# Early transposes of h0: a four-layer graph network on one Trainium2 core, with 64 small transposes moved to its start

## The chip, the cores and the metric

The kernel runs on 1 core of one Trainium2 chip. The metric is the device time of one execution in microseconds (us), and the kernel before takes 1860.86 us, the median of 3 runs (1860.08 to 1861.27). Its engines are named as the profile names them: PE does matmuls (PEld loads their weights), DVE is VectorE, ACT is ScalarE, POOL is GpSimd, and SP issues most transfers (its rows are named SPq). Each works through its own instructions in order.

## The reference

6,250 nodes with 128 features, 206,250 edges sorted by their target (every node has a loop), and four graph layers in a row, each added to x. What matters here is the first:

```python
h = jnp.maximum(_layernorm(x, axis=-1), 0.0)
msg = edge_weight[:, None] * h[src]
neighbor = segment_sum(msg, dst, num_segments=6250)
interaction = h * neighbor
out = neighbor @ W1.T + b1 + interaction @ W2.T + b2
x = x + leaky_relu(out, 0.2)
```

The second layer takes the mean of the neighbours' normed rows, the third a mean over another table's rows by the same edges, the fourth a gated recurrent cell on the neighbours' sum. All use the same edges, so one dense matrix of edge counts serves them.

## The kernel before, in words

The nodes are padded to NB = 49 blocks of 128. The edges are turned into dense matrices, and every sum over neighbours is then a matmul. The kernel has four parts.

**The head.** x is loaded in groups of GB = 4 blocks, normed in place into the tile h0 (128 rows x 49 blocks x 128 features, kept on the chip), and the edges of the first strip are fetched. `normed(n)` (L894) does n groups' norms.

**The strips.** 25 strips of SB = 2 blocks of target nodes (`strip`, L938; the last has one block). A strip has 32 *counts* (`count`, L766). A count is 24 bf16 matmuls (L781) of one-hot columns (`one_hots`, L747, DVE) into a PSUM tile pK, and two ACT copies out of it: L790 writes the edge counts as bytes to `cnt`, L788 the summed edge weights to `edge_w`. Finished counts are stored to DRAM (`cnt_d`, L969) for the later layers. `edge_w` is 49 x 256 f32 a partition. Strips take it in turn from two pools of one buffer each, edge0 for even strips and edge1 for odd ones (L940).

Between the counts of strip k stands the work of earlier strips, as generators that the loop calls at fixed places (the tables END_AT, EDGES_AT, NORMS_AT in L932 to L936). The instructions run in exactly this order, because `manual_schedule` (L886) is on:
- `layer0(k-1)` (L810): the first layer's sum, h0 times `edge_w`, as f32 matmuls of half the rows each into the two PSUM tiles pB and pM (L818). It comes in 16 *turns*, one after every second count. Then ACT copies pB to `agg` (L826) and DVE adds pM (L827).
- `finish0(k-2)` (L842), a strip's *end*: `turned_rows` (L833) transposes h0's two blocks as four 64 x 64 pieces (L839) into a PSUM tile pt. DVE multiplies it by `agg` into `inter` (L848). Eight matmuls by W1 and W2 (L855, L856) follow, then bias, leaky relu, the next norm, four transposes of the new rows h1 by the same L839, and a matmul (L876). h1, the new x and that product go to DRAM (h_d, u_d, f_d).

The small tiles of the ends (agg, inter, xs0, full, h1, ht0, fs) come from the pool `work` (L614), which is opened ahead of edge0 and edge1 (L615), pay, hot, cnts, turned and once (L633, L634). So their size decides at which address the others begin. After the last strip the remaining turns of `layer0` run by themselves, with the last full strip's end spread between them (L1008 to L1012).

**The dense layers.** The strips' pools are closed with their `with` block. New pools take the same space from its start: late, work, late2, ring (3 buffers), wide (3), early, whole (4), in L1016 to L1022. Layer 2's `dense` (L1025) works in steps of five blocks of source nodes. In `bring` (L1031), SP loads byte counts into a `ring` tile (L1051, 640 KB for two steps), DVE (L1066) and ACT (L1064) widen them to `wide`, a row for each block, and PE multiplies each row by the block's `parts`, the high and low half of h1 (L1088, two matmuls a row). `parts` is filled by `h_up_to` (L1136): POOL loads a group of h1 from h_d into one of four `h` tiles of the pool whole (L1141), DVE casts it to the high half (L1151), and the low half is a subtraction on DVE or, from group 7 on, POOL (L1152).

The scheduler decides how these late instructions stand between those of the last strips. One that writes space of a closed pool waits for the last reader of what lay there.

Of the kernel before, what the change touches and what calls it, by code (L numbers as in the profile page):

```python
# [488 lines left out]
NPR = -(-NB // 2)  # L489
NBP = 2 * NPR  # L490
KP = 5
KQ = 5
NSMP = -(-E // P)
TOP = 1 << 13
# [5 lines left out]
def fast(ctx: ExitStack, tc: tile.TileContext, a: dict, out: bass.AP, flag: bass.AP):  # L500
# [33 lines left out]
    f_d = dram.tile([P, NB, D], F32, name="f_d")  # L534
    h_d = dram.tile([P, NB, D], F32, name="h_d")
    x_d = dram.tile([P, NB, D], F32, name="x_d")
    smp_d = dram.tile([NSMP, 1], I32, name="smp_d")

    def rows(table, g, nb):
# [57 lines left out]
    with ExitStack() as bx:  # L597
# [149 lines left out]
        def one_hots(by_edge, t0):  # L747

            of = slice(t0 // TI, t0 // TI + tq)
            keys, parts = (t[:, of, :, None, :] for t in by_edge)  # L750

            def at(i, n):
                return keys[:, :, i].to_broadcast([P, tq, n, TI])

            def count_up(n):
                return iota[:, None, :n, :].to_broadcast([P, tq, n, TI])

            s_hot = hot.tile([P, tq, P, TI], BF16, name="s_hot")
            nc.vector.tensor_tensor(s_hot, count_up(P), at(0, P), op=ALU.is_equal)  # L759
            k_hot = hot.tile([P, tq, 4, NBP, TI], BF16, name="k_hot")  # L760
            nc.vector.tensor_tensor(k_hot[:, :, 0], count_up(NBP), at(1, NBP), op=ALU.is_equal)  # L761
            nc.vector.tensor_tensor(k_hot[:, :, 1:, :NB], k_hot[:, :, :1, :NB].to_broadcast([P, tq, 3, NB, TI]),  # L762
                                    parts.to_broadcast([P, tq, 3, NB, TI]), op=ALU.mult)
            return s_hot, k_hot
# [45 lines left out]
        def layer0(k, nb, edge_w):  # L810

            g, w = k * SB, nb * P
            pl = [psum.tile([P, 512], F32, name=n) for n in ("pB", "pM")]
            for i in range(turns0):
                for s in range(i * NB // turns0, (i + 1) * NB // turns0):
                    for h in range(WN):
                        r = slice(h * H, (h + 1) * H)
                        nc.tensor.matmul(pl[h][:, :w], h0[r, s, :], edge_w[r, s, :w], start=s == 0,  # L818
                                         stop=s == NB - 1)
                if i + 1 < turns0:  # L820
                    yield
            if k == NS - 1:
                ends.append(pl)
                return
            agg = work.tile([P, SW], F32, name="agg")
            nc.scalar.copy(agg[:, :w], pl[0][:, :w])  # L826
            nc.vector.tensor_add(agg[:, :w], agg[:, :w], pl[1][:, :w])  # L827
            ends.append(finish0(g, nb, agg))

        def by_half(t, nb):  # L830
            return t[:, : nb * P].rearrange("p (b h c) -> p h b c", h=WN, c=H)

        def turned_rows(t, nb):  # L833

            pt = banks.tile([P, WN, 512], F32, name="pt", tag="pK")
            for j in range(nb):
                for h in range(WN):
                    r = slice(h * H, (h + 1) * H)
                    nc.tensor.transpose(pt[:, h, j * H : (j + 1) * H], t[r, j, :], ident[r, r])  # L839
            return pt[:, :, : nb * H].rearrange("p h (b c) -> p h b c", c=H)  # L840

        def finish0(g, nb, agg):  # L842

            w = nb * P
            queue = nc.sync if g < (NS - 3) * SB else nc.gpsimd
            pt = turned_rows(h0[:, g : g + nb, :], nb)
            inter = work.tile([P, SW], F32, name="inter")
            nc.vector.tensor_mul(by_half(inter, nb), by_half(agg, nb), pt)  # L848
            xs = work.tile([P, SB, D], F32, name="xs0", bufs=2)
            load_x(xs, g, nb)  # L850
            yield
            po = banks.tile([P, SW], F32, name="po", tag="pK")
            for j in range(nb):
                s = slice(j * P, (j + 1) * P)
                nc.tensor.matmul(po[:, s], agg[:, s], w1, start=True, stop=False)  # L855
                nc.tensor.matmul(po[:, s], inter[:, s], w2, start=False, stop=True)  # L856
            full = work.tile([P, SW], F32, name="full")
            nc.vector.tensor_add(full[:, :w].rearrange("p (b f) -> p b f", f=D),
                                 po[:, :w].rearrange("p (b f) -> p b f", f=D), bcast(b12, nb))
            nc.vector.scalar_tensor_tensor(full[:, :w], full[:, :w], 0.2, full[:, :w],  # L860
                                           op0=ALU.mult, op1=ALU.max)
            nc.vector.tensor_add(flat(xs[:, :nb, :]), flat(xs[:, :nb, :]), full[:, :w])
            h1 = work.tile([P, SB, D], F32, name="h1")
            yield from norm(xs, h1, nb)
            nc.gpsimd.tensor_tensor(xs[:, :nb, :], xs[:, :nb, :], h1[:, :nb, :], op=ALU.add)
            queue.dma_start(h_d[:, g : g + nb, :], h1[:, :nb, :])
            queue.dma_start(u_d[:, g : g + nb, :], xs[:, :nb, :])
            yield
            pt = turned_rows(h1, nb)
            ht = work.tile([P, SW], F32, name="ht0")  # L870
            nc.scalar.copy(by_half(ht, nb), pt)
            yield
            pf = banks.tile([P, SW], F32, name="pf", tag="pK")
            for j in range(nb):
                s = slice(j * P, (j + 1) * P)
                nc.tensor.matmul(pf[:, s], ht[:, s], wr, start=True, stop=True)  # L876
            fs = work.tile([P, SB, D], F32, name="fs")
            nc.vector.tensor_add(fs[:, :nb, :], pf[:, :w].rearrange("p (b f) -> p b f", f=D),
                                 bcast(bl, nb))
            queue.dma_start(f_d[:, g : g + nb, :], fs[:, :nb, :])  # L880
# [13 lines left out]
        def normed(n):  # L894
            for _ in range(2 * n):
                next(norming)

        first = prepare(0)
        next(first)
        normed(4)  # L900
        next(first)
        normed(1)
        next(first)
# [22 lines left out]
        by_edge = next(first)  # L926
        next(norming)
        hots = one_hots(by_edge, 0)
        before, ends, turns, edges = iter(()), [], turn(), prepare(1)


# [6 lines left out]
        def strip(k, nb):  # L938
            nonlocal before, edges, by_edge, hots
            edge_w = edge[k % 2].tile([P, NB, SW], F32, name="edge_w")  # L940
            end = ends.pop() if ends else iter(())
            last, piece, following = nb * P // WN, 0, None
            for w0 in range(0, last, PW):
                if w0 % TW == 0:
                    if k < 2 and piece in NORMS_AT[k]:
                        next(norming, None)
                    if not k and piece in FIRST_AT:
                        following = next(edges, None)
                    now, t1 = hots, w0 + TW
                    if t1 < last:  # L950
                        hots = one_hots(by_edge, t1)
                    elif following:
                        hots = one_hots(following, 0)
                if w0 // PW % PT == PT // 2:
                    if piece in END_AT:
                        next(end, None)
                    if k < 2 and piece in NORMS_AT[k]:
                        next(norming, None)
                    if k and piece in EDGES_AT:
                        following = next(edges, None)  # L960
                if w0 * WN % P == 0:
                    cnt = cnts.tile([P, NPR, P], U16, name="cnt")
                count(w0, now, cnt, edge_w)
                if k and w0 // PW % 2:
                    next(before, None)
                g, w1 = k * SB + w0 * WN // P, w0 + PW
                if w1 * WN % P == 0:
                    c, i = CHUNK_OF[g]
                    nc.sync.dma_start(cnt_d[c, :, i, :], flat(cnt))  # L969
                if w1 % (PW * PT) and w1 < last:  # L970
                    continue
                if piece == (NEXT_AT if k else FIRST_AT[-1]) and k + 2 < NS:
                    edges = prepare(k + 2)
                    next(edges)
                for _ in range(TURN_AT.count(piece) if k else 0):
                    next(turns, None)
                piece += 1
            by_edge = following
            for _ in before:
                next(end, None)  # L980
            for _ in end:
                pass
            before = layer0(k, nb, edge_w)
# [601 lines left out]
```

## Time and profile before

| what | value |
|---|---|
| runs, median of 3 | 1860.86 us |
| the profiled execution, its own time | 1859.0 us |
| its span (first to last instruction) | 1857.2 us |
| granted PE clock | 0.994 |
| PE busy | 1791.2 us (96%) |
| DVE, ACT, POOL busy | 1381.6, 1208.7, 471.6 us |
| L818, the first layer's sums | 4900 matmuls, 1237.0 us on two row halves that run side by side |
| L781, the counts | 18816 matmuls, 404.5 us |
| L1088, the dense layers | 2548 matmuls, 574.3 us |
| L839, the transposes in the ends | 192, median 219 ns |

The time is 1.8 us above the span of the same execution. Busy time of one engine can overlap that of another. Two row halves of PE also overlap, so PE's busy time is not the sum of its rows. A profile row reads: line, engine, operation, the tile written, an arrow, the tiles read, the count, then the shape.

### The profile page before, as it was taken

The numbers are of one execution on the slowest core, as the hardware profiler recorded it, in microseconds if no ns is written. First come the engines' busy times: TensorE is split into PE (matmuls) and PEld (weight loads), VectorE is DVE, ScalarE is ACT, GpSimd is POOL, SyncE is SP. The second block draws the span as 40 slices with busy tenths as digits, with TensorE's granted clock in tenths as the row PEclk, the third lists the DMA queues.
The fourth block names the chain that finished last, engine by engine and source line by source line (L and its number), as shares of the span: only waits on it lengthen the run. The fifth ranks groups of instructions, "written<-read, shape, count | busy, mean of one in ns | idle before, by whom it ended". The sixth has DMA issues, their size and how long they took to land. (4 is left out here: it accounts for less than half of the span.)

```text
span 1857.2 us, 65339 instructions
## 1 busy us (share of the span) xinstructions
PE 1791.2 (96%) x28191; PEld 1521.2 (82%) x28191; DVE 1381.6 (74%) x2946; ACT 1208.7 (65%) x2835; POOL 471.6 (25%) x431
## 2 busy tenths in 40 slices
PE   2799999999999999999999999999999999999997
PEld 2688888888888888888888888888888877787776
DVE  7878888888888888888886777777787755454444
ACT  6777777777777777777774677777565654443443
POOL 2333333433334333334332111111122210000000
PEclk9899999999999999999999999999999999999999
DMA  4245454644644544545223555554555444344342
GB/s 106 58 123 115 101 139 106 129 126 100 136 106 118 122 103 126 117 99 132 72 79 117 179 173 162 167 154 124 143 155 147 139 148 142 121 136 148 121 140 60
DMA packets 262513, 231.72 MB, mean 125 GB/s; under 512 B 101518, under 2 KB 246424, under 8 KB 262215
## 3 DMA queue, kind: packets, MB, share of 16 engines
q1 hardware_dynamic: 253415, 210.67, 42.4%
q0 software_dynamic: 8800, 16.78, 3.2%
q8 instruction: 223, 3.65, 0.8%
q14 instruction: 75, 0.61, 0.1%
HBM read 130.37 MB, written 76.54 MB: 111 GB/s over the span
## 5 line engine op out<-in xcount | busy, mean ns | idle before, releaser
L818 PE MATMUL pM<-edge_w,h 64*128 64x256 f32 (+1 forms) x2450 | 619.2, 387 | 0.2
L818 PE MATMUL pB<-edge_w,h 64*128 64x256 f32 (+1 forms) x2450 | 617.8, 387 | 0.7 <-ACT agg L826 0.3
L1088 PE MATMUL acc<-wide,parts 128*128 128x512 f32 (+2 forms) x2548 | 574.3, 383 | 2.7 <-DVE wide L1066 1.3
L1088 PEld LDWEIGHTS acc<-wide,parts 128*128 128x128 f32 x2548 | 460.0, 188 | 101.2 <-issue 10.5
L790 ACT CAST cnt<-pK 128x400 uint8<-128x400 f32 x784 | 394.9, 504 | 222.5 <-PE pK L781 187.4
L781 PEld LDWEIGHTS <-s_hot 64*128 64x128 bf16 x18816 | 382.9, 95 | 80.5 <-issue 21.5
L818 PEld LDWEIGHTS pB<-edge_w,h 64*128 64x128 f32 x2450 | 421.6, 187 | 31.5 <-issue 3.3
L781 PE MATMUL pK<-k_hot,s_hot 64*128 64x49 bf16 (+1 forms) x18816 | 404.5, 192 | 32.2 <-DVE k_hot L762 19.2
L818 PEld LDWEIGHTS pM<-edge_w,h 64*128 64x128 f32 x2450 | 421.6, 187 | 5.4 <-issue 2.9
L788 ACT COPY edge_w<-pK 128x392 f32<-128x392 f32 x784 | 397.0, 506 | 0.0
L759 DVE TENSOR_TENSOR s_hot<-iota,keys 128x2048 bf16<-128x2048 bf16 x196 | 240.7, 1228 | 85.5 <-remote 52.5
L762 DVE TENSOR_TENSOR k_hot<-k_hot,by_edge 128x2352 bf16<-128x2352 bf16 x196 | 271.6, 1386 | 8.4
L1066 DVE TENSOR_SCALAR_CACHE_REDUCE wide<-ring 128x512 fp32r<-128x512 uint8 (+2 forms) x325 | 193.4, 651 | 25.3 <-issue 15.6
L1064 ACT ACTIVATE wide<-ring 128x512 fp32r<-128x512 uint8 (+2 forms) x312 | 184.7, 595 | 24.3 <-ACT wide L1064 19.6
L639 POOL DMA_INDIRECT dst<-in_dst,off_i x50 | 84.1, 1682 | 360.7 <-DVE node L702 341.6
L1058 ACT CAST wide<-ring 128x1024 fp32r<-128x1024 uint8 (+3 forms) x130 | 120.7, 957 | 70.6 <-PE acc L1088 65.7
L1057 DVE CAST wide<-ring 128x1536 fp32r<-128x1536 uint8 (+2 forms) x130 | 119.6, 945 | 53.4 <-PE acc L1088 41.5
L1088 PE MATMUL acc<-wide,q_parts 128*128 128x512 f32 (+2 forms) x650 | 157.3, 392 | 1.2 <-DVE wide L1043 0.9
L1088 PEld LDWEIGHTS acc<-wide,q_parts 128*128 128x128 f32 x650 | 115.6, 188 | 28.5 <-DVE wide L1043 3.1
L761 DVE TENSOR_TENSOR k_hot<-iota,keys 128x800 bf16<-128x800 bf16 x196 | 112.4, 573 | 0.0
L1429 POOL DMA_DIRECT2D out<-x x12 | 10.2, 853 | 322.9 <-DVE x L1426 293.1
L639 POOL DMA_INDIRECT line<-in_dst,at_i x24 | 40.9, 1703 | 163.2 <-DVE at_i L675 155.3
(246 smaller groups left out, 1650.3 us busy)
## 6 DMA issues: line engine op xcount, KB each, us to landing
ring<-cnt_d SPq DMA_DIRECT2D x110, 640.0 KB
cnt_d<-cnt SPq DMA_DIRECT2D x49, 800.0 KB
cntT_d<-tt SPq DMA_DIRECT2D x125, 160.0 KB
ring<-cntT_d SPq DMA_DIRECT2D x60, 320.0 KB
ring<-cnt_d SPq DMA_DIRECT2D x10, 480.0 KB
ring<-cnt_d SPq DMA_DIRECT2D x10, 320.0 KB
h<-in_x SPq DMA_DIRECT2D x12, 256.0 KB
xs<-in_x SPq DMA_DIRECT2D x24, 128.0 KB
```

The costliest lines, as they stand in the source:

```text
L639: nc.gpsimd.indirect_dma_start(out=t, out_offset=None, in_=col[name], in_offset=bass.IndirectOffsetOnAxis(ap=idx, axis=0))
L759: nc.vector.tensor_tensor(s_hot, count_up(P), at(0, P), op=ALU.is_equal)
L762: nc.vector.tensor_tensor(k_hot[:, :, 1:, :NB], k_hot[:, :, :1, :NB].to_broadcast([P, tq, 3, NB, TI]), parts.to_broadcast([P, tq, 3, NB, T ...
L781: nc.tensor.matmul(pk[:, h, to], s_hot[r, u, :, t], rhs, start=j == 0, stop=True, skip_group_check=True)
L788: nc.scalar.copy(m.rearrange("p b (i h) -> p b i h", h=WN), by_block[:, 1, :NB])
L790: nc.scalar.copy(m.rearrange("p b e (i h) -> p b e i h", h=WN), by_block[:, 0].rearrange("p (b e) i h -> p b e i h", e=2))
L818: nc.tensor.matmul(pl[h][:, :w], h0[r, s, :], edge_w[r, s, :w], start=s == 0, stop=s == NB - 1)
L1057: nc.vector.tensor_copy(*(v[:, :3].rearrange("p k b n -> p b k n") for v in (to, of)))
L1058: nc.scalar.copy(to[:, 3:ks], of[:, 3:ks])
L1064: one = nc.scalar.activation(to[:, k], of[:, k], AF.Copy, accum_out=total)
L1066: one = nc.vector.tensor_scalar(to[:, k], of[:, k], 1.0, None, op0=ALU.mult, op1=ALU.add, accum_out=total)
L1088: nc.tensor.matmul(acc[:, : nb * P], parts[:, s, j, :], rhs, start=s + j == 0, stop=s == end and j == 1)
```

## The change

With EARLY = 8, the transposes of h0 for the first 8 groups (32 blocks, those of strips 0 to 15) are done ahead:
- `turn_early(g)` transposes a group's four blocks, each as one 128 x 128 matmul, into a PSUM tile under the tag pK. ACT copies the 128 x 512 result to a new tile h0T (two buffers in `work`), and it returns a function that has SP store it to the new DRAM tensor h0T_d (256 KB).
- Groups 0 and 1 are done in the head after `normed(4)`, and stored after the first one-hots. Groups 2 to 7 are done in strip 0, one in each of its pieces 0 to 5, at the second count of the piece, and stored at once.
- `layer0(k)` for strips 0 to 15 begins with a load of the strip's two transposed blocks (128 KB, SP) into a new tile ht_in (two buffers in `work`). `finish0` multiplies `agg` by that tile and leaves out its four h0 transposes. Strips 16 to 24 work as before.

The pool `work` grows by the four new buffers, two of 2 KB and two of 1 KB in each partition.

```diff
+EARLY = 8
+    h0T_d = dram.tile([P, NB, P], F32, name="h0T_d")
 def layer0(k, nb, edge_w):
             pl = [psum.tile([P, 512], F32, name=n) for n in ("pB", "pM")]
+            ht = None
+            if g + nb <= EARLY * GB:
+                ht = work.tile([P, SW], F32, name="ht_in", bufs=2)
+                nc.sync.dma_start(ht, h0T_d[:, g : g + nb, :].rearrange("p b n -> p (b n)"))
...
-            ends.append(finish0(g, nb, agg))
+            ends.append(finish0(g, nb, agg, ht))
+        def turn_early(g):
+
+            nb = min(GB, NB - g)
+            p = banks.tile([P, WN, 512], F32, name="pt", tag="pK")
+            for j in range(nb):
+                nc.tensor.transpose(p[:, 0, j * P : (j + 1) * P], h0[:, g + j, :], ident)
+            ht = work.tile([P, GB * P], F32, name="h0T", bufs=2)
+            nc.scalar.copy(ht[:, : nb * P], p[:, 0, : nb * P])
+            return lambda: nc.sync.dma_start(h0T_d[:, g : g + nb, :].rearrange("p b n -> p (b n)"), ht[:, : nb * P])
-        def finish0(g, nb, agg):
+        def finish0(g, nb, agg, ht=None):
...
-            pt = turned_rows(h0[:, g : g + nb, :], nb)
             inter = work.tile([P, SW], F32, name="inter")
-            nc.vector.tensor_mul(by_half(inter, nb), by_half(agg, nb), pt)
+            if ht is None:
+                pt = turned_rows(h0[:, g : g + nb, :], nb)
+                nc.vector.tensor_mul(by_half(inter, nb), by_half(agg, nb), pt)
+            else:
+                nc.vector.tensor_mul(inter, agg, ht)
         normed(4)
+        kept = [turn_early(g * GB) for g in range(2)]
...
         hots = one_hots(by_edge, 0)
+        for store in kept:
+            store()
 def strip(k, nb):
...
+                if not k and w0 // PW % PT == 1:
+                    turn_early((piece + 2) * GB)() if piece + 2 < EARLY else None
```

## The prediction

> **What bounds the kernel now.** I read the page's shares first, then busy time by windows, then the timeline of each engine around the places that the change touches. PE is the bound:
>
> ```profile
> PE 1791.2 (96%) x28191; PEld 1521.2 (82%) x28191; DVE 1381.6 (74%) x2946; ACT 1208.7 (65%) x2835; POOL 471.6 (25%) x431
> ```
>
> By windows (columns: length, then busy time of PE, PEld, DVE, ACT, POOL, then clock, DMA share, GB/s), the start is not bound by PE and the strips are:
>
> ```profile
> 0.00:60.00 60.00, 21.96 (x654) 19.39 (x655) 49.87 (x181) 37.24 (x99) 22.71 (x29) 0.95 0.40 99
> ...
> 500.00:600.00 100.00, 99.90 (x2540) 88.32 (x2538) 85.40 (x159) 73.56 (x180) 34.83 (x29) 1.00 0.49 113
> ```
>
> So PE work removed from a strip is time saved, and work added to strip 0 is mostly hidden (PE is idle for 17.2 of that strip's 41.2 us). The transposes concerned:
>
> ```profile
> L839 PE MATMUL pt<-f_ident,h x192: 216/219/227, 114.8 to 1013.0; 64*128 64x64 f32 x192
> ```
>
> **What the removed transposes cost.** 219 ns is the time of one alone; they overlap with each other and with their neighbours. So I compare turns, from a turn's first pB matmul to the next turn's, in the timeline of PE:
>
> ```profile
> 193.83 0.46 PE L818 MATMUL pB<-edge_w,h 64*128 64x256 f32 x1
> 194.12 0.48 PE L818 MATMUL pM<-edge_w,h 64*128 64x256 f32 x1
> ...
> 195.21 0.28 PE L839 MATMUL pt<-f_ident,h 64*128 64x64 f32 x2
> ...
> 196.33 0.46 PE L818 MATMUL pB<-edge_w,h 64*128 64x256 f32 x1
> ...
> 198.52 0.46 PE L818 MATMUL pB<-edge_w,h 64*128 64x256 f32 x1
> ```
>
> The first of these turns holds h0's four transposes and takes 2.50 us; the second holds none and takes 2.19 (over the trace the medians are 2.503 and 2.175). The difference is 0.33 us, but pM starts 0.29 us after pB where 0.09 is usual: it waits for DVE to add the last pM into `agg` (L827), and that stays. So 0.33 - 0.20 = 0.13 is the transposes'. Turns with h1's four transposes, which have no such wait, have a median of 2.311, 0.136 more. I take 0.12 for a strip, 16 x 0.12 = **-1.9 us**. The ends are 0 and 16 x 0.33 = 5.2. `inter` by DVE from PSUM is 414 ns (L848), a like product of two SBUF tiles 426 ns (L862): no change, and DVE is not the bound there.
>
> **What is added at the start.** 32 full transposes: 8 in the head, where PE waits, and 24 in strip 0. The trace has none of this shape. The nearest row is the turn with the eight 128 x 128 matmuls of L855 and L856: median 3.459 us, 1.28 more than a plain one, so 0.64 for four and 6 x 0.64 = 3.9 us for strip 0. Its 17.2 us of idle time hides that; I take 0, with 0 and 3.9 as ends (an addition cannot gain). A rule in the Trainium skill, "TensorEngine Tiling (Array Packing)", Key Properties, speaks against it: a change of tiling mode drains the engine, and each early group would change it twice. The 0.64 already has such a change in it, so by the rule the sum stays as it is where the idle time covers it and is 3.9 higher where not.
>
> ACT gets eight copies, priced by a copy of the same shape:
>
> ```profile
> L1371 ACT COPY wc<-pT 128x512 f32<-128x512 f32 x11 | 6.4, 586 | 16.6 <-PE pT L1369 16.6
> ```
>
> 8 x 0.586 = 4.7 us, beside 22.8 us in which ACT idles in the first 60. SP issues 8 stores and 16 loads more, about 0.4 to 0.6 us of its queue each, beside a DMA share of about one half. A store in strip 0 waits on SP for its ACT copy; behind it stand `cnt_d` stores and x loads that nobody needs for some 10 us or more. A load is issued a strip ahead of its use. All of that 0.
>
> **What moves: addresses.** `work` grows by 2 x 2 KB + 2 x 1 KB = 6,144 bytes a partition, and every strip pool behind it starts that much higher. The late pools don't move. In the built programs, edge0 lies at bytes 67,552 to 117,728 before and 73,696 to 123,872 after; edge1 follows it, to 167,904 and 174,048. The first `ring` buffer starts at 123,360, `parts` at 169,440, the `h` buffers lie from 219,616 on. So after the change:
> - the first `ring` buffer shares 512 bytes with edge0, which strip 24 uses. Before, it lay in edge1 alone, free after strip 23.
> - the first blocks of `parts` lie over edge1 (before: over one-hots and smaller tiles).
> - the `h` buffers lie over scratch tiles that the strips use until strip 23; before they were over nothing.
>
> In the built order, SP's first ring load and the first `wide` casts now wait for the very last `layer0` matmul (pM, 128 wide), and the splits of h1 wait for strip 23's last one. In the trace of before those times were used. Timelines of SP, DVE and PE:
>
> ```profile
> 1003.12 1.32 SPq L1051 DMA_DIRECT2D ring<-cnt_d  x2
> ```
> ```profile
> 994.91 0.43 DVE L1151 CAST parts<-h 128x512 fp32r<-128x512 f32 x1 [8.96 <-DMA cnt_d<-cnt]
> ...
> 1010.38 0.16 DVE L575 SCALAR_TENSOR_TENSOR f_shift<-f_mv,f_rstd 128x2 f32<-128x2 f32 x1
> 1010.58 0.69 DVE L1066 TENSOR_SCALAR_CACHE_REDUCE wide<-ring 128x512 fp32r<-128x512 uint8 x1
> ...
> 1018.61 3.62 DVE L1151 CAST parts<-h 128x512 fp32r<-128x512 f32 x4
> 1022.15 0.67 DVE L1066 TENSOR_SCALAR_CACHE_REDUCE wide<-ring 128x512 fp32r<-128x512 uint8 x1
> ```
> ```profile
> 1017.46 0.27 PE L818 MATMUL pM<-edge_w,h 64*128 64x128 f32 x1
> 1017.66 4.85 PE L1088 MATMUL acc<-wide,parts 128*128 128x512 f32 x20
> ```
>
> The ring loads were issued at 1003, the first rows widened from 1010.6, and PE went from its last `layer0` matmul to layer 2 without a gap. Three terms follow.
>
> 1. *Splits in the way of the last end.* DVE did seven pairs of L1151 and L1152 and one cast more from 994.91 to 1003.7, before the last end needed it. After, all of them stand behind the add of `agg` at 1003.6, between the steps of that end. A pair is 1.07 us (994.91 to 995.98), so 7.5 x 1.07 = 8.0 us. DVE's idle times there (1.09, 2.06 and 0.27 us) take 3.4 of it. `f_shift` comes 4.6 later, and so do ACT's two rows of h1, which ended at 1011.50. PE's transposes of h1 were due at 1012.98, 1.5 later. So PE, which works in order, stands for 4.6 - 1.5 = **+3.1**.
> 2. *The ring load in the open.* After the last pM matmul (its end 1017.73, plus term 1): 0.1 to issue, the load, 0.68 for the first row. By the packet records the ring loads issued alone at 1036.06, 1041.06, 1046.16, 1051.52 and 1060.82 landed 4.34 to 4.49 us later. 0.1 + 4.4 + 0.7 = **+5.2**. The Trainium skill, "DMA: Bandwidth & Descriptors", Anatomy of one DMA, fits 2.0 us plus bytes over 436 GB/s (for POOL's path; this one is SP's): 3.5 us for 655,360 bytes, which would make the sum 0.9 lower; the trace's 4.4 decides.
> 3. *Step 3.* Two steps were ready at 1017.66 and gave PE 4.85 us. After, DVE has five rows to do once the load has landed (5 x 0.61), the add and product for the last block (0.6), four casts (3.6), then the first row of step 3 (0.67): 7.9 us after landing. PE ends step 2 at 0.7 + 4.85 + 0.15 = 5.7. **+2.2**.
>
> PE is busy for all of 1030 to 1060 before, so nothing later wins this back. Ends for the three: 0 for terms 1 and 3 if the scheduler's order leaves DVE time that I don't see; 5.2 for the load is firm within 0.3 if it waits at all.
>
> **Sum.** -1.9 + 0 + 3.1 + 5.2 + 2.2 = +8.6 us. On the profiled execution's own time, 1859.0 + 8.6 = 1867.6; that execution is 1.9 under the median of the runs, so the runs should give 1860.86 + 8.6 = **1869.5**.
>
> **Rivals.**
> - *Only the ring load is late* (terms 1 and 3 hidden, or one of them small): -1.9 + 5.2 = +3.3 to +5.5, 1864.2 to 1866.4. For it: DVE had idle time in that stretch. Against: it is 3.4 us for 8.0 of work.
> - *Strip 0 is dearer*: the six groups cost their 0.64 each, or ACT's copies hold the PSUM buffers that the counts need: up to +3.9, 1873.4. For it: three buffers serve counts, early transposes and norms, and ACT paces parts of strip 0. Against: 17.2 us idle.
> - *Not slower: the gate is open by then.* Place: the first ring load on SP. If the 512 shared bytes do not hold it, or strip 24's readers of them are done early, the loads go out at 1003 as before, the splits find room, and only the saving is left: 1859.0, price 0. It decides for issues before about 1008, since landing (4.4), casts and the last `layer0` matmul at 1017.7 leave that much. Against: the built order has the wait on the last matmul.
> - *The transposes are worth their rows*: 64 x 0.219 = 14.0 us, net 10.5 - 14.0 = -3.5, 1857.4 or less. It needs over 0.66 us a strip; a turn's whole difference is 0.33.
> - That the change does not do what it says is excluded: 64 transposes fewer and 32 more are in the built order.
>
> **Chances.** Forecast (1866.5 to 1872.5) 0.66; ring load alone 0.14; strip 0 dearer 0.10; gate open 0.07; rows' worth 0.03. 0.2% is 3.7 us, about what a measurement of this kernel can tell from no change: faster ends at 1857.1 and slower begins at 1864.6. Half of the second case falls within: faster 0.03, same 0.07 + 0.07 = 0.14, slower 0.83. Leaving out the gate's case, the rows' case and half of strip 0's, the range is 1862.5 to 1874.5; the random stalls of PE beside POOL's gathers (2 to 3 us at 51.7 and 86.6) can move with the code and are within it.
>
> **What would show it.** L839 has 128 matmuls of 64 x 64; strips 2 to 17 are about 0.12 us shorter; ACT has eight new 128 x 512 copies in the first 67 us and strip 0 is not longer. SP's first ring load comes after the last `layer0` matmul, PE is idle 5 us ahead of the first layer 2 matmul, and about 3 us ahead of the last h1 transposes, with the casts of `parts` after the add of `agg`. If that load is issued at about 1003, the prediction is wrong.

## The result and the profile after

The changed kernel takes 1883.91 us (median of 4 runs, 1878.19 to 1887.33), the kernel before beside it 1861.07: the ratio is 1.0122, with a 95% interval of 1.0104 to 1.0140. Forecast were 1869.5 and a range of 1862.5 to 1874.5. So the sign was right and the size far off: +22.8 us instead of +8.6. The profiled execution took 1881.6 us, 22.6 over that of before; its span is 1879.6, which is 22.4 more.

PE has hardly more work (page, first part), but the start stands still (busy time by windows; columns as before):

```profile
PE 1797.6 (96%) x28159; PEld 1525.1 (81%) x28159; DVE 1381.2 (73%) x2946; ACT 1209.9 (64%) x2843; POOL 465.3 (25%) x431
```
```profile
0.00:60.00 60.00, 22.84 (x497) 17.94 (x499) 40.81 (x157) 32.71 (x86) 15.96 (x23) 0.82 0.44 116
...
500.00:600.00 100.00, 99.49 (x2520) 88.24 (x2514) 87.04 (x156) 74.66 (x184) 32.97 (x30) 1.00 0.51 124
```

In the first 60 us DVE does 40.8 us of work where it did 49.9, ACT 32.7 for 37.2. I cut the span at each strip's first copy into `edge_w` and at the first layer 2 matmul:

| stretch (us) | before | after | difference |
|---|---|---|---|
| head | 25.96 | 25.94 | 0.0 |
| strip 0 | 41.19 | 52.48 | +11.3 |
| strip 1 | 46.57 | 47.07 | +0.5 |
| strips 2 to 23 | 859.06 | 861.62 | +2.6 |
| of this, PE idle | 6.19 | 12.08 | +5.9 |
| strip 24 to the first layer 2 matmul | 44.89 | 52.60 | +7.7 |
| from there to the end | 839.54 | 839.92 | +0.4 |

**Strip 0** holds half of it, and the timelines of ACT, SP, DVE and PE say why:

```profile
25.94 0.49 ACT L790 COPY edge_w<-pK 128x392 f32<-128x392 f32 x1
39.76 0.58 ACT L855 COPY h0T<-pt 128x512 f32<-128x512 f32 x1 [13.33 <-DMA h0T_d<-h0T]
40.24 0.50 ACT L792 CAST cnt<-pK 128x400 uint8<-128x400 f32 x1
```
```profile
29.24 0.58 SPq L933 DMA_DIRECT2D smp<-smp_d  x1
...
34.87 0.26 SPq L554 DMA_DIRECT2D last_x<-in_x  x1
36.78 18.07 SPq L856 DMA_DIRECT2D h0T_d<-h0T  x6
```
```profile
30.43 0.17 DVE L570 TENSOR_SCALAR f_std<-f_mv 128x4 f32<-128x4 f32 x1
41.26 0.18 DVE L575 RECIPROCAL f_rstd<-f_std 128x4 f32<-128x4 f32 x1 [10.66 <-ACT f_std L572]
```
```profile
40.40 1.63 PE L783 MATMUL pK<-k_hot,s_hot 64*128 64x99 bf16 x48 [12.39 <-ACT h0T L855]
```

h0T has two buffers, and groups 0 and 1 fill both in the head, by 14.6 us. Group 2's copy, in strip 0's first piece, must write the first of them again. Its store has not gone out: it stands on SP behind the load of `smp`, which waits until 29.24 for a transfer of its own, and behind seven small loads. It is issued at 36.78, and the copy runs at 39.76. ACT works in order, so the counts' copies and the square root of a norm wait behind that copy, and DVE waits for the root, and PE for both. PE's wait of 12.39 us ends with the copy itself, since that frees a PSUM buffer under the tag pK. ACT's wait of 13.3 us costs 11.3: before, ACT idled for 8.5 us of that strip.

**After the strips** the picture is the one forecast: no ring load before the last `layer0` matmul, and two gaps of PE.

```profile
1033.52 1.31 SPq L1075 DMA_DIRECT2D ring<-cnt_d  x2
```
```profile
1028.31 0.66 PE L845 MATMUL pt<-f_ident,h 64*128 64x64 f32 x4 [1.24 <-ACT h L581]
1030.96 0.71 PE L895 MATMUL pf<-f_WrT,ht 128*128 128x128 f32 x4
1039.71 7.48 PE L1112 MATMUL acc<-wide,parts 128*128 128x512 f32 x20 [6.27 <-DVE wide L1090]
```

The same twenty matmuls that took 4.85 us take 7.48 now. The rows of DVE and ACT do not hold them back: two rows, enough for four matmuls, come every 0.6 us, while the matmuls start 0.43 us apart where 0.23 is usual. What changed is the clock that the profile shows as granted to PE. At the same matmuls it was 1.00 before; it fell in PE's wait and is 0.50 for 6.8 us (columns as before):

```profile
1038.50:1045.30 6.80, 5.59 (x13) 4.42 (x14) 6.11 (x16) 5.43 (x18) 1.99 (x2) 0.50 0.73 223
```

That costs next to nothing here. PE is done with the twenty at 1047.19, and DVE ends its first row of step 3 at 1047.00, so step 3 would have waited for DVE anyway (the padded kernel below shows it).

The transposes number 128 (`L845`, below) instead of 192, and the median of a turn that held h0's falls from 2.503 to 2.379 us.

```profile
L845 PE MATMUL pt<-f_ident,h x128: 216/221/273, 150.3 to 1028.7; 64*128 64x64 f32 x128
```

### The profile page after: what moved, and what is told of

Same layout as the page of the kernel before. It is cut to its first block, busy times and chain, and to the rows that moved or that the text cites. A ratio compares the mean times of both kernels' runs of the same rounds, so it can differ in the third digit from the quotient of the medians.

```text
span 1879.6 us, 65343 instructions
## 1 busy us (share of the span) xinstructions
PE 1797.6 (96%) x28159; PEld 1525.1 (81%) x28159; DVE 1381.2 (73%) x2946; ACT 1209.9 (64%) x2843; POOL 465.3 (25%) x431
## 5 line engine op out<-in xcount | busy, mean ns | idle before, releaser
L1112 PEld LDWEIGHTS acc<-wide,parts 128*128 128x128 f32 x2548 | 462.2, 189 | 107.5 <-issue 10.5
L1112 PEld LDWEIGHTS acc<-wide,q_parts 128*128 128x128 f32 x650 | 115.6, 188 | 28.3 <-DVE wide L1067 2.8
L1453 POOL DMA_DIRECT2D out<-x x12 | 10.2, 851 | 322.9 <-DVE x L1450 293.1
```

Source lines behind the costliest of these rows:

```text
L1112: nc.tensor.matmul(acc[:, : nb * P], parts[:, s, j, :], rhs, start=s + j == 0, stop=s == end and j == 1)
```

## The experiments

They ran in five sessions. The kernels of a session shared a chip, and each is compared with the kernel before in that session. Sessions differ: before takes 1838.7 to 1839.3 in two of them and 1859.0 to 1863.7 in the other three. The chip's number does not make that difference: the sessions of 1839.3 and of 1859.0 ran on the chip of the same number. Stretches are cut as in the table above.

**1. The two losses apart.** Four kernels, in a session where before takes 1839.3.

*Stores first*: the kept stores ahead of the load of `smp`, in the changed kernel.

```diff
+        for store in kept:
+            store()
         nc.sync.dma_start(smp, smp_d.rearrange("s o -> o s").to_broadcast([P, NSMP]))
...
-        for store in kept:
-            store()
```

> Of the changed kernel's 22.4 us in span, strip 0 has 11.3, the part after strip 24's begin 8.1, and strips 1 to 23 the rest. Theory: strip 0 is lost because ACT's copy for group 2 waits 13.3 us for a buffer of h0T, whose store stands on SP behind the load of smp and six more. With the two kept stores ahead of that load, the wait is gone; a shorter one can remain for group 4, whose buffer's store still stands behind them (0 to 3 us). Strip 0 takes 42 to 45 us instead of 52.5, and the time is 1872 to 1877. Rival: the early transposes and copies hold the three pK buffers that the counts need; then strip 0 stays above 49 us and the time above 1880.

Measured: +11.5 us over before (ratio 1.0061, interval 1.0044 to 1.0078). Strip 0 takes 45.6 us. ACT's wait for group 2 has shrunk to 9.15 us; that it would vanish was wrong. The stores were issued at 25.29 and 28.02 (which took SP 2.6 and 3.5 us), and their packets moved only from 30.3 to 35.4, behind x loads of 512-byte packets.

*Pad only*: the kernel before with 6,144 unused bytes.

```diff
         work = pool("work", 1)
+        pad = work.tile([P, 1536], F32, name="pad")
+        nc.gpsimd.memset(pad[:, :1], 0.0)
```

> The kernel before with an unused tile of 6,144 bytes in the pool work, nothing else. Theory: the addresses alone cost the 8.1 us after the strips, so 1868 to 1870; the first ring load goes out after the last layer0 matmul, and strip 0 takes 41.2 us as before. Rival: that loss is from the added transfers, or the scheduler meets the addresses without cost; then 1861.

Measured: +9.2 us (1.0050, 1.0033 to 1.0067). Nothing of the change is in it, and it shows both gaps:

```profile
995.76 0.66 PE L841 MATMUL pt<-f_ident,h 64*128 64x64 f32 x4 [1.10 <-ACT h L579]
```
```profile
1007.10 6.30 PE L1090 MATMUL acc<-wide,parts 128*128 128x512 f32 x20 [6.22 <-DVE wide L1068]
```

Here the granted clock is 0.50 for less of the twenty matmuls, which take 6.30 us. Still step 3 starts 7.38 us after the first of them, against 5.22 before: 2.16 later, after PE has waited 0.63 us for DVE's row. In the changed kernel step 3 starts 2.46 later; step 4 starts 2.15 later here and 2.16 there. So it is DVE's work that sets this delay, as forecast, and not the slower matmuls.

*Own pool*: the changed kernel with h0T and ht_in where they move no other tile.

```diff
         cnts, turned, once = pool("cnts", 2), pool("turned", 3), pool("once", 1)
+        ahead = pool("ahead", 1)
-                ht = work.tile([P, SW], F32, name="ht_in", bufs=2)
+                ht = ahead.tile([P, SW], F32, name="ht_in", bufs=2)
-            ht = work.tile([P, GB * P], F32, name="h0T", bufs=2)
+            ht = ahead.tile([P, GB * P], F32, name="h0T", bufs=2)
```

> The changed kernel with h0T and ht_in in a pool of their own, opened last of the strips' pools, so that edge0, edge1 and all others lie where they lay before. Theory: the 8.1 us after the strips go, strip 0 stays at 52.5: 1874 to 1877, and the first ring load is issued about 15 us ahead of the first layer 2 matmul. Rival (transfers, not addresses): 1882 to 1885.

Measured: +7.8 us (1.0048, 1.0031 to 1.0065). Strip 0 keeps 49.6 us, and ACT waits 13.11 us for the store again. The ring loads go out at 988.36, before the last `layer0` matmul, and from strip 24 to the first layer 2 matmul it is 47.8 us, against 52.7 in the padded kernel.

*Both edits*, and three h0T buffers:

```diff
-                ht = ahead.tile([P, GB * P], F32, name="h0T", bufs=2)
+                ht = ahead.tile([P, GB * P], F32, name="h0T", bufs=3)
```

> Both edits at once, with three h0T buffers instead of two. Theory: both losses go and only the saving of 16 times 0.124 = 2.0 us and about 1 us in strip 0 are left, beside the random stalls of PE in the strips (6 to 12 us in the two profiles, their cause open): 1858 to 1864. Rival (pK buffers held by the early transposes): 1870 or more, with strip 0 above 49 us.

Measured: -0.8 us by the medians (ratio 1.0001, 0.9991 to 1.0011): level with before. Strip 0 takes 43.4 us, 45.1 pass from strip 24 to the first layer 2 matmul, and ACT's longest wait for a store is this one:

```profile
35.68 0.58 ACT L856 COPY h0T<-pt 128x512 f32<-128x512 f32 x1 [3.64 <-DMA h0T_d<-h0T]
```

So the two losses are separate and have these two causes. How much of the shorter wait is due to the third buffer and how much to the earlier stores, this kernel does not tell; the earlier stores alone left 9.15 us. A plain strip without the transposes takes 38.09 us here and 38.21 with them.

**2. Which bytes.** This and the next three kernels ran where before takes 1861.7.

```diff
-        pad = work.tile([P, 1536], F32, name="pad")
+        pad = work.tile([P, 1408], F32, name="pad")
```

> The kernel before with an unused tile of 5,632 bytes instead of 6,144: edge0 ends exactly where the first ring buffer begins, while the splits of h1 stay behind strip 23's last matmul. Theory: the part of the ring load goes (its wait is 512 bytes wide), and the splits' part stays, PE's wait ahead of the last h1 transposes, 1.2 us in the changed kernel: 1 to 3 us over before, against 9.2 with 6,144 bytes. If the loss is from the splits or the moved addresses in general, it stays at 8 to 9.

Measured: +12.4 us (1.0061, 1.0042 to 1.0080), so the time speaks against the theory; its parts do not. From strip 24 to the first layer 2 matmul it is 49.45 us, against 52.73 with 512 bytes more and 44.89 before (from two other sessions). The ring loads go out early, and PE goes from `layer0` to layer 2 without a gap. What is left is the splits, dearer than I expected (timelines of SP and PE):

```profile
1013.37 1.31 SPq L1053 DMA_DIRECT2D ring<-cnt_d  x2
```
```profile
1026.21 0.66 PE L841 MATMUL pt<-f_ident,h 64*128 64x64 f32 x4 [2.91 <-ACT h L579]
...
1030.06 0.71 PE L878 MATMUL pf<-f_WrT,ht 128*128 128x128 f32 x4 [1.12 <-ACT ht L873]
```

With the ring loads in flight, the h tiles land later (DVE waits 1.72 us for one), and the splits hold PE for 2.91 + 1.12 us instead of 1.24. Step 3 again starts 1.7 us later than before. Most of the rest lies in strips 2 to 23 (868.5 us, 19 PE stalls, against 859.1 and 858.1 in the two profiles of before, of other sessions), see part 3.

The changed kernel, with no edit:

> The changed kernel again, on the chip that these runs share. If the parts add, it is 9.2 (addresses) plus 7.8 + 2 (the kept buffer, with the saving taken out) less 2, about 17 to 23 us over before. If the 6 us of added PE stalls between strips 2 and 23 of the first profile come from the change, those strips sum to more than in the kernel before here too; if they belong to the chip, they sum to about 2 us less.

Measured: +28.3 us (1.0152, 1.0122 to 1.0183), more than the parts. Strip 0 51.3, strip 24 to layer 2 52.7, strips 2 to 23 869.5 with 24 stalls. In a third run beside a profile of before it was +24.0 (1.0139, 1.0109 to 1.0169; 2 runs), and strip 0 took 53.7 us against 44.3.

The own pool, three h0T buffers, and:

```diff
-        kept = [turn_early(g * GB) for g in range(2)]
+        for g in range(2):
+            turn_early(g * GB)()
```

> h0T and ht_in in their own last pool, three h0T buffers, and the stores of groups 0 and 1 issued right behind their copies in the head. Theory: the copy of group 3 no longer waits for a store (3.6 us in the run with both edits) and the load of smp is not delayed; strip 0 takes 41 to 43 us and the time is 1 to 3 us under before. Rival: the early transposes hold pK buffers, strip 0 stays at 43 to 44 and the time equals before.

Measured: +14.0 us (1.0074, 1.0050 to 1.0098). The two stores move at 14.5 to 16.8 us, and the gather of the first strip's edge weights lands later: POOL goes on at 20.81 us, in the changed kernel at 18.89. So the head takes 27.85 us, 1.9 more. Strip 0 takes 40.6, as in the two kernels of that session that add nothing to it (40.9 and 41.4): its loss is gone, and the rival of the pK buffers falls. The rest of the time is lost in strips 2 to 23, 875.1 us with 29 stalls.

The kernel before with less work:

```diff
-            pt = turned_rows(h0[:, g : g + nb, :], nb)
+            if g + nb <= 8 * GB:
+                nc.vector.tensor_mul(inter, agg, agg)
+            else:
+                pt = turned_rows(h0[:, g : g + nb, :], nb)
```

> The kernel before with h0's transposes left out for strips 0 to 15 (agg times agg in their place), nothing added: the whole of what the change could save. By the turns (2.503 to 2.379 us) 16 times 0.124 = 2.0 us less than before. If the transposes cost their rows, 7 to 14 less; if they are hidden, 0.

Measured: +4.5 us (1.0014, 0.9995 to 1.0033), though it only leaves work out. Strips 2 to 23 took 869.3 us, with 25 stalls.

**3. The stalls.** A stall here is a gap over 0.45 us between the starts of two PE rows, the second a count's. The trace shows no releaser for them ("issue"), and they stand beside POOL's gathers: in the second run of both edits all 29 lie within 0.3 us of one, while gathers fill about a quarter of these strips (236 of 879 us). Timelines of PE and POOL in that run:

```profile
646.22 0.23 PE L784 MATMUL pK<-k_hot,s_hot 64*128 64x99 bf16 x4 [0.47 <-issue]
646.96 0.19 PE L784 MATMUL pK<-k_hot,s_hot 64*128 64x49 bf16 x1 [0.51 <-issue]
```
```profile
645.38 0.98 POOL L642 DMA_INDIRECT src<-in_src,off_i  x1 [0.30 <-issue]
646.66 0.95 POOL L642 DMA_INDIRECT wgt<-in_edge_weight,off_i  x1 [0.30 <-issue]
```

Four kernels of above, with no new edit:

> The kernel before, profiled on the chip that the next three share, since chips differ: on one it takes 1839, on another 1862. Strips 2 to 23 and PE's idle time in them are what the others are compared with. If the idle time in the strips belongs to the chip, it is as large here as in the changed kernel (within 2 us); if the change brings it, it is about 6 us less here.

> Both edits again (own last pool, three h0T buffers, kept stores ahead of the smp load), on another chip. Theory: within 0.2% of before (-1 to +2 us), strip 0 at 43 to 44. If added transfers bring PE stalls in the strips, 5 us or more over before.

> The kernel before with h0's transposes left out for strips 0 to 15 (agg times agg instead), again: the first run of it came out 4.5 us over before, on a chip with many PE stalls. By the turns it is 2.0 us under before. If it is again over before, moving the program alone costs PE stalls, since nothing is added here.

> The changed kernel beside the profile of before on the same chip: strip 0 +10 to +11.5, the part from strip 24 to the first layer 2 matmul +7.7, strips 2 to 23 -2.0 apart from PE's stalls; sum 17 to 20 where stalls are alike, more where the changed kernel stalls more.

Measured (before 1863.7), strips 2 to 23 alone: before 858.1 us and 11 stalls; both edits 878.9 and 29, time +13.2 (1.0070, 1.0046 to 1.0094); left out 866.9 and 26, time +4.3 (1.0025, 1.0007 to 1.0044); changed 866.3 and 21. So the kernel with both edits is level where PE stalls seldom and slower where it stalls often. Leaving work out is slower there too, so added transfers can't be the whole cause.

The stalls cost more than PE's idle time. With clusters of them the granted clock falls to 0.50 for 3.4 or 6.8 us, as here after the two stalls above:

```profile
650.40:657.20 6.80, 6.13 (x111) 5.51 (x111) 3.34 (x4) 4.12 (x11) 2.11 (x5) 0.50 0.73 153
```

In strips 2 to 23 this adds up to 20.5 us in the second run of both edits, and to 3.4 to 13.7 in eight other profiles with 19 stalls or more (of parts 2 and 3). It is 0 in the first profile of the changed kernel, in those of before and its moved versions, and in the sessions of 1839. With half of that time as lost, both edits should take 14.2 (more idle time of PE) + 10.2 - 2.0 (the transposes) = 22.4 us more than before in these strips; measured 20.9. For the kernel with the transposes left out it is 7.8 + 5.1 - 2.0 = 10.9; measured 8.9. So the stalls and what follows them are nearly all of this loss, with a cause still open.

Does the place of the code decide? 64 or 96 one-column matmuls in the head move all later PE instructions:

```diff
         normed(4)
+        fill = banks.tile([P, WN, 512], F32, name="fill", tag="pK")
+        for _ in range(64):
+            nc.tensor.matmul(fill[:1, 0, :1], ident[:, :1], ones[:, :1], start=True, stop=True)
```

> The kernel before with 64 one-column matmuls more in the head, where PE waits, on a PSUM tile that nobody reads. They move all later instructions of PE in the program and do nothing else. Theory of the stalls: PE stalls for its instructions beside POOL's gathers, and which strips it hits depends on where the code lies; then the stalls fall into other strips than 3 and 14, and on a chip with many stalls the time moves by several us, up or down. Rival: the stalls come from the changes' transfers or waits; then this is the kernel before, within 0.2%.

> The same with 96 matmuls: by the theory another set of strips and another sum; by the rival no change.

> Both edits (own last pool, three h0T buffers, kept stores ahead of the smp load) with the 64 matmuls in the head. Without them this was 0.8 us under before on one chip and 13.2 over on another, where PE stalled 29 times for 15.8 us in strips 2 to 23. If the place of the code decides, stalls and time differ from that by several us; if the added transfers do it, it is again about 13 over on such a chip.

> The same with 96 matmuls. On a chip with few stalls all four stand within 0.2% of before.

Measured (before 1859.0): the kernel before +0.7 (1.0005, 0.9993 to 1.0017) with 9 stalls, and -1.9 (0.9992, 0.9980 to 1.0004) with 3. Both edits +8.9 (1.0054, 1.0037 to 1.0070) with 25, and +12.4 (1.0071, 1.0047 to 1.0096) with 26. Moving the code changed where before stalls: strip 3, its longest of strips 2 to 23 (41.6 and 41.4 us in its two profiles), takes 38.9 and 38.8, and with 64 matmuls strips 2 and 20 take 40.5 and 41.0. It does not explain how often: 9 and 3 stalls against 25 and 26. So the theory may hold for the place of a stall, and falls for their number.

Last, four short matmuls in place of h0's transposes, to give a strip its count of PE instructions and PSUM banks back:

```diff
+                few = banks.tile([P, WN, 512], F32, name="few", tag="pK")
+                for j in range(nb):
+                    for h in range(WN):
+                        r = slice(h * H, (h + 1) * H)
+                        nc.tensor.matmul(few[:H, h, j : j + 1], ident[r, r], ident[r, r][:, :1], start=True, stop=True)
```

> The kernel before with h0's transposes left out for strips 0 to 15 (agg times agg instead), and in their place four matmuls of one column into a PSUM bank that nobody reads: as many PE instructions and the same turn of the PSUM banks as before, but less PE time and no wait of DVE for PE. Without the four, PE stalled 26 times in strips 2 to 23 and the time was 4.3 us over before. If the count of PE instructions in a strip (or the turn of the banks) decides where PE stalls, the stalls fall back to 3 to 11 and the time is 0 to 2 us under before. If it is that DVE and POOL run ahead when they do not wait for the transposes, the stalls stay at 20 or more and the time 3 us or more over.

> Both edits (own last pool, three h0T buffers, kept stores ahead of the smp load), with the same four short matmuls in the ends of strips 0 to 15. Without them 13.2 us over before on a chip with many stalls, with 25 to 29 stalls. If the count of PE instructions in a strip or the turn of the banks decides: stalls 3 to 11, time within 0.2% of before or up to 2 us under it, and this is the version to keep. If the transfers or the missing wait bring the stalls: 8 us or more over before again.

Measured (before 1838.7): +4.8 (1.0026, 1.0016 to 1.0035) and +6.5 (1.0033, 1.0021 to 1.0046), with 4 and 3 stalls. PE stalled seldom in their session, so these two do not decide the question. The slowdown is the short matmuls' own: PE's records show eight for the four, and the median of the turn that holds them is 2.911 us where the transposes' was 2.503. A later turn of the strip (that of W1 and W2) gets 0.09 shorter, so a plain strip takes 38.53 us, 0.32 more than with the transposes and 0.44 more than without (38.21 and 38.09, in the other session of 1839). 16 x 0.32 = 5.1 us, against the 4.8 measured; 16 x 0.44 = 7.0, against 7.3 from -0.8 (both edits) to +6.5.

**What stays open** is what makes PE stall. In the sessions of 1859 and more and in the first profiles it was 10 and 11 times in before, 9 and 3 in its moved versions, and 19 to 29 times in every other kernel, one that only pads the memory among them. Neither the place of the code nor the transfers explain all of these, and the instruction count was not decided. In the two sessions of 1839 (six kernels profiled, 3 to 5 stalls) it plays no part. What makes that difference between sessions, the runs do not tell; two of them, one of each kind, were on the chip of the same number. No version tried beats before beyond its interval.

## Why the prediction was wrong, point by point

- **The failed step is that of the added copies and stores**: "8 x 0.586 = 4.7 us, beside 22.8 us in which ACT idles in the first 60", and of the stores "All of that 0". I asked who waits behind a store on SP, and not what the store itself waits behind, nor who waits for it to release its buffer. I listed `cnt_d` stores behind it; in front of it stood the load of `smp`, which the trace of before shows at 29.00 us, ahead of seven loads up to 33.4. Two buffers, both filled by 14.6, and a third copy due at about 26: a wait of at least 7 us was to be read there. Measured: 13.3 us of wait, and strip 0 +11.3 us, for a term that I had put at 0. Without it the time would have been about 1872.6, inside the range. In the third run, beside a profile of before, strip 0 is 9.4 longer (before's own strip 0 took 41.2 and 44.3 us in its two profiles).
- The rival "strip 0 is dearer" had the right stretch, half a mechanism and a wrong price, up to 3.9. A PSUM buffer is what PE waits for (12.39 us), but it is held because ACT's copy out of it waits for a store, and of that the rival says nothing. The groups' matmuls take 0.66 to 1.18 us for four where I had 0.64, 5.8 us in all in strip 0, and are mostly inside PE's idle time as forecast: with the store's wait mostly gone, strip 0 takes 43.4 us, against 42.4 in the padded kernel of the same session.
- **The saving**, 0.12 a strip and 1.9 us, was right: 2.503 to 2.379 us a turn, and 38.21 to 38.09 for a plain strip.
- **The addresses** were right as a mechanism, shown by the pad alone and, for the ring's 512 bytes, by taking them away. Predicted 10.5 us; measured 9.2 for the pad. Term by term, in the changed kernel: the splits 1.24 us for 3.1 (4.6 from strip 24 on in the kernel with 5,632 bytes, where the ring loads run beside them), the ring load 6.27 for 5.2 (ACT and DVE start on it 5.4 us after its issue, where I had 4.4 for the landing), step 3 2.5 for 2.2, and step 4 2.2. That nothing later wins this back is true of the dense layers (still 1.75 at the last of their `acc` matmuls), but what follows them was 1.4 us shorter in this execution, for a reason that is open; so the stretch after the first layer 2 matmul grew by 0.4 alone. The rival of the open gate fell: the load went out at 1033.52. DVE's end came 2.8 us later, not 4.6 (and 2.8 less the 1.5 of slack is the 1.3 or so that PE stood): I took the whole length of the splits and only the visible idle time off, but the end's short dependent steps had more room between them.
- **The stalls** were in the range as "2 to 3 us that can move". In the first profile PE idled 5.9 us more in strips 2 to 23, with 20 stalls for 10, and the changed kernel's runs spread over 9 us where before's spread over 3. It came again in both later runs of the changed kernel (24 and 21 stalls against 11); why, nothing here shows.

The sum as it came: strip 0 +11.3, strip 1 +0.5, strips 2 to 23 +2.6 (-2.0 by the transposes, so +4.6 from elsewhere, where PE's idle time is 5.9 more), then +7.7 and +0.4: 22.5, against 22.4 of the span. Where stalls are few, the parts add too: +11.5 with the addresses and what was left of the store's wait, +7.8 with the store's wait alone, -0.8 with neither.

## What to carry to other kernels

A new store that frees a buffer is two waits: read what stands ahead of it on its queue, and count the buffers until the first one is written again. A new tile in a pool that opens early moves every pool behind it; where later pools take the same space, look up which tile of the old ones ends up under their first loads, and put the new tile last. A part that the sum leaves at nothing because the engine has idle time needs the order of that engine's work checked as well: idle time does not help an instruction that stands behind a waiting one.

## What the runs showed of the hardware

- A store's issue on SP can itself take long: in the first run of both edits the two kept stores, issued at 22.98 us behind x loads that were still moving, held SP for 5.86 and 1.01 us, until 29.95, and their packets moved from 30.1. The same issue in strip 0 took 0.34 us.
- PE's granted clock fell from 1.00 to 0.50 for 6.8 us in one wait of 6.27 us (changed kernel), and 20 times in strips 2 to 23 of nine profiles, for 3.4 or 6.8 us, with clusters of stalls: in the 3.4 us ahead of each fall PE had idled for 0.9 to 2.1 us in all (1.44 in the first run with the transposes left out, from stalls at 601.7 and 602.7). One cluster of three, in before at 172.3 to 174.0, brought no fall. At 0.50, f32 matmuls of 512 columns started 0.43 us apart instead of 0.23.
- Four f32 matmuls of one column on 64 rows cost a turn 0.41 us more than the four 64 x 64 transposes that they replaced (2.911 against 2.503), and a strip 0.32 more (38.53 against 38.21).
- The same program is 20 us apart between sessions (1839, and 1859 to 1864), with plain strips of 38.2 and 38.75 us; the granted clock of the profiled runs was 0.98 to 1.00 in both.
